# Projecting a whole batch ahead of attention, and putting the experts' spare tiles behind a branch

## The chip, the cores and the metric

One core of a Trainium2 chip runs one program. The metric is the device time of one execution in microseconds (us); less is better. Every time below comes from the runs or the profile of the kernel before.

## What is computed

The reference is one transformer layer with adaptive normalisation, for 4 sequences ("batches") of 2048 tokens with 256 channels, all in fp32:

```python
mod = (silu(c) @ wmod).reshape(4, 6, 1, 256)     # sa, ca, ga, sb, cb, gb; ga and gb at least 0.25 in size
h = layernorm(x) * (1 + ca) + sa
x = x + ga * attention(h)                        # 16 heads of 16 channels, rotary, causal softmax
h = layernorm(x) * (1 + cb) + sb
x = x + gb * moe(h)
# moe: sigmoid scores of 16 experts, the best 2 of 4 groups, the best 4 experts in them, weights scaled by 2.5;
#      y = sum over the 4 experts of w2(silu(w1 h) * (w3 h)) * weight, and a shared expert of the same shape (192 inner)
```

## The kernel before

**Attention.** Tokens go in blocks of 512, four to a batch (NQ = 4), 16 in all. For each block, `prologue(n)` normalises the rows of x, transposes them, multiplies by the modulation, projects to q, k and v (TensorE, PE), turns q and k by the rotary table, splits them into a high and a low part (fp32r) and stores them in DRAM (qd, kd, vd). A unit of attention is a block of queries with a group of 4 heads (`units`: 16 to a batch; the first batch has its units one by one, the later ones in pairs). For each unit `row_max` computes the scores once for the maximum of each row (VectorE, DVE, reduces them), and the main loop computes them again, transposed, in steps of 128 keys: PE (L1139, L1146), the exponential on ScalarE (ACT, L1154), on the diagonal a causal select on GpSimd (POOL, L1158), and the product with v on PE (L1087).

The order of instructions on PE, ACT, DVE and POOL is written out by hand; DMAs issued by SyncE (SP) are ordered by the framework. Everything beside the main loop is written as generators that yield what they need (a PSUM bank, DVE time, POOL time). The main loop pulls pieces of them between its steps, through queues (`Background`): `ahead` holds the prologues of blocks to come, at a rate set by `due`, so that a block is there when its first unit needs it; `maxes` the row maxima of the next unit; `ends` the output projection (`finish`); `after` the sending of finished blocks to the experts (`send`), and last `find_tiles`.

Only block 0 is projected at once, in an inner function `opening` of `prologue(0)`. Ahead of it stand the constants, the modulation and its rows (`rows`, `rowd`, L241 to L253) in a pool of their own, which is released before the pools of attention are filled. Blocks 1 to 3 go through `ahead`, beside the first units. Between the two, 32 regions of the buffers for the experts are filled with zeros (L1045, 272 KB each).

**Sending.** `send` normalises a finished block, routes it, and scatters each token's row to the regions of its four experts (L477). Experts work on tiles of 256 rows (TT), two tiles ("a pair") at a time, each tile of one expert; `find_tiles` counts the tiles and writes a table with each tile's expert and first row. There are two phases: blocks 0 to 11, whose experts' work may start when attention ends, and blocks 12 to 15, which are sent beside the first phase's pairs.

**Experts.** The number of pairs is fixed when the kernel is built, for the most padding that there can be, 255 rows an expert:

```python
self.pairs = -(-((4 * self.tokens + E * (TT - 1)) // TT) // 2)   # 56 in phase 0, 24 in phase 1
```

A pair that the table doesn't fill works on a repeated tile, and its results go to rows that nobody reads. Each pair loads 2 x 640 KB of weights (L1224) and 2 x 272 KB of rows (L1226), turns the rows (`turn`, L1240), multiplies up (`inner_a`, `inner_b`, L1255), takes silu times gate on ACT and DVE, multiplies down (`outer`, L1293 and L1304), scales by the weight and scatters four times 128 rows (`give`, L1358). Between these parts the loop pulls pieces of other work:

```python
def other(n):
    (late if m < split else rest).pull(n)      # called as other(2), other(1), other(2) for each pair
```

`late` is the sending of phase 1's blocks; `rest` (`back`) is, for all 16 blocks, the shared expert (`shared`, L1398) and, for the 12 blocks of phase 0, the sum of the four experts' results (`combine`, L1443 to L1450). After the last pair `rest` is drained, and the last four blocks are collected (L1386) and combined.

Of the kernel before, what the change touches and what calls it, by code (L numbers as in the profile page):

```python
# [118 lines left out]

@with_exitstack  # L120
def adaln_attention_moe(
# [33 lines left out]
    nc.sync.dma_start(gwT, gate_w)  # L155
    gbias = const.tile([P, E], F32, name="gbias")
    nc.sync.dma_start(gbias, gate_bias.partition_broadcast(P))
    bef = const.tile([P, E, E], F32, name="bef")
    nc.sync.dma_start(bef, before.partition_broadcast(P))

    sml = const.tile([P, 2 + len(PHASES), E], F32, name="sml")
    nc.sync.dma_start(sml, small.partition_broadcast(P))
    befb = const.tile([P, E, E], BF, name="befb")
    nc.vector.tensor_copy(befb, bef)
# [14 lines left out]
    for k, ph in enumerate(phases):  # L179


        ph.xs = dram.tile([E * ph.region, ROW], F32, name=f"xs{k}")

        ph.yd = dram.tile([4 * ph.tokens + 2 * ph.pairs * TT, D], F32, name=f"yd{k}")
        ph.first = sml[:, 2 + k, :]

        ph.run = const.tile([P, E], F32, name=f"run{k}")
        nc.vector.tensor_copy(ph.run, ph.first)
        ph.name = str(k)
# [16 lines left out]
    def gate(pool, g, name):  # L206

        sign = pool.tile(list(g.shape), F32, name=f"sign{name}")
        nc.vector.tensor_scalar(sign, g, 0.0, 2.0, ALU.is_ge, ALU.mult)
        nc.vector.tensor_scalar_add(sign, sign, -1.0)  # L210
        mag = pool.tile(list(g.shape), F32, name=f"mag{name}")
        nc.vector.tensor_scalar_mul(mag, g, -1.0)
        nc.vector.tensor_max(mag, mag, g)
        nc.vector.tensor_scalar_max(mag, mag, 0.25)
        nc.vector.tensor_mul(g, sign, mag)

    with tc.tile_pool(name="modw", bufs=1) as mw, tc.tile_pool(
        name="modp", bufs=1, space=PSUM
    ) as mp:
        wm = mw.tile([P, 2, 6 * D], F32, name="wm")  # L220
        nc.sync.dma_start(wm, wmod.rearrange("(k p) n -> p k n", p=P))
        sg = mw.tile([P, 2, B], F32, name="sg")
        nc.scalar.activation(sg, cT, AF.Sigmoid)
        nc.vector.tensor_mul(sg, sg, cT)
        pm = mp.tile([P, 4, B], F32, name="pm")
        for m in range(4):
            for k in range(2):
                nc.tensor.matmul(
                    pm[:, m, :],
                    lhsT=wm[:, k, m * P : (m + 1) * P],  # L230
                    rhs=sg[:, k, :],
                    start=(k == 0),
                    stop=(k == 1),
                )
        nc.vector.tensor_copy(mod, pm)
        nc.vector.tensor_scalar_add(mod[:, 2:4, :], mod[:, 2:4, :], 1.0)
        rows = mw.tile([B, 4, D], F32, name="rows")
        for m in range(4):
            pr = mp.tile([B, D], F32, name=f"pr{m}")
            for k in range(2):  # L240
                nc.tensor.matmul(  # L241
                    pr,
                    lhsT=sg[:, k, :],
                    rhs=wm[:, k, (2 + m) * D : (3 + m) * D],
                    start=(k == 0),
                    stop=(k == 1),
                )
            nc.vector.tensor_copy(rows[:, m, :], pr)
        nc.vector.tensor_scalar_add(rows[:, 2, :], rows[:, 2, :], 1.0)
        gate(mw, rows[:, 0, :], "a")  # L250
        gate(mw, rows[:, 3, :], "b")
        rowd = dram.tile([B, 4 * D], F32, name="rowd")
        nc.sync.dma_start(rowd, rows.rearrange("b m d -> b (m d)"))  # L253
# [8 lines left out]
    def normalise(xb, pools, xn):  # L262
# [11 lines left out]
        yield 0, 0, 0  # L274
# [22 lines left out]
    def route(lg, tp):  # L297
# [20 lines left out]
        def ranks(v, k, allowed):  # L318
# [20 lines left out]
            yield 0, 0, 0  # L339
# [32 lines left out]
    def send(n, xp, tp, psum, tag):  # L372
# [13 lines left out]
        for _ in range(3):  # L386
            yield 0, 0, 0
        h = yield from normalise(xb, tp, xb)
# [6 lines left out]
        yield 0, 0, 0  # L395
# [7 lines left out]
        yield 0, 0, 0  # L403
# [11 lines left out]
        re, ch, w = yield from route(lg, tp)  # L415
# [3 lines left out]
        yield 0, 0, 0  # L419
# [69 lines left out]
    tabs = ctx.enter_context(tc.tile_pool(name="tabs", bufs=1))  # L489

    def find_tiles(ph):
# [70 lines left out]
        nc.vector.tensor_scalar_add(tab[:, :, 2], tab[:, :, 2], -5.0)  # L562
        tabi = tabs.tile([P, 2, 3], I32, tag="tabi", name="tabi")
# [21 lines left out]
    with ExitStack() as actx:  # L585
# [24 lines left out]
        wqkv = acst.tile([P, 2, 3 * D], F32, name="wqkv")  # L610
        nc.sync.dma_start(wqkv, qkv_w.rearrange("(k p) n -> p k n", p=P))
        bqkv = acst.tile([P, 3 * D], F32, name="bqkv")
        nc.sync.dma_start(bqkv, qkv_b.partition_broadcast(P))
        wo = acst.tile([P, 2, D], F32, name="wo")
        nc.sync.dma_start(wo, out_w)
        ob = acst.tile([P, D], F32, name="ob")
        nc.sync.dma_start(ob, out_b.partition_broadcast(P))
        rp = acst.tile([P, T // P, 2, 2, HD // 2], F32, name="rp")
        nc.sync.dma_start(rp, rope)
# [12 lines left out]


        va_new = acst.tile([P, NG, 4, VG], F32, name="va")
        vh = va_new[:, :, :, : 4 * (HD + 1)].rearrange("p g t (h e) -> p g t h e", e=HD + 1)
        nc.gpsimd.memset(va_new, 0.0)
        for g in range(NG):
            nc.gpsimd.memset(vh[:, g, :, :, 0:1], 1.0)

        def prologue(n):  # L640
# [38 lines left out]
            def opening(hT, high_low, store):  # L679


                full = [P, 2 * H, 2, HD // 2]
                qks, rots = {}, {}

                def project(t):
                    ps = psp.tile([P, 2, BT], F32, tag="s", name="first")
                    for to, cols in ((ps[:, 0], slice(0, 2 * D)), (ps[:, 1, :D], slice(2 * D, 3 * D))):
                        for k in range(2):
                            nc.tensor.matmul(
                                to,  # L690
                                lhsT=hT[:, k, t * P : (t + 1) * P],
                                rhs=wqkv[:, k, cols],
                                start=(k == 0),
                                stop=(k == 1),
                            )
                    qk = ep.tile([P, 2, BT], F32, tag="e", name="qk0")
                    nc.vector.tensor_add(qk[:, 0], ps[:, 0], bqkv[:, : 2 * D])
                    nc.vector.tensor_add(
                        vh[:, :, t, :, 1:],
                        ps[:, 1, :D].rearrange("p (g h e) -> p g h e", g=NG, e=HD),  # L700
                        bqkv[:, 2 * D :].rearrange("p (g h e) -> p g h e", g=NG, e=HD),
                    )
                    qks[t] = qk

                def rotate(t):
                    qk = qks.pop(t)
                    parts = qk[:, 0].rearrange("p (h e two) -> p h e two", e=HD // 2, two=2)
                    prod = []
                    for s, eng in enumerate((nc.gpsimd, nc.vector)):
                        r_ = tp.tile(full, F32, tag=f"r{s}", name=f"r{s}", bufs=1)  # L710
                        eng.tensor_tensor(
                            r_,
                            parts[:, :, :, s].unsqueeze(2).to_broadcast(full),
                            rp[:, t, s].unsqueeze(1).to_broadcast(full),
                            ALU.mult,
                        )
                        prod.append(r_.rearrange("p h a e -> p h (a e)"))
                    xr = qk[:, 1].rearrange("p (h d) -> p h d", d=HD)
                    nc.vector.tensor_add(xr, prod[0], prod[1])
                    rots[t] = xr  # L720

                def split(t):
                    xr = rots.pop(t)
                    pt = wps.tile([P, 4, P], F32, tag="w", name="ptq")
                    for c_ in range(4):
                        nc.tensor.transpose(
                            pt[:, c_, :],
                            xr[:, 8 * c_ : 8 * c_ + 8, :].rearrange("p h d -> p (h d)"),
                            ident,
                        )  # L730
                    cols, whole = high_low(t, pt)
                    high, low = parts_[0]
                    lower(cols, whole, high, low)
                    if t % 2:
                        store(t // 2, high, low)

                project(0)
                project(1)
                rotate(0)
                project(2)  # L740
                for t in range(4):
                    if t < 3:
                        rotate(t + 1)
# [763 lines left out]
    for n in phases[1].blocks[:2]:  # L1507
        collect(n)
# [77 lines left out]
```

## Time and profile before

| | us |
|---|---|
| median of 3 runs (lowest, highest) | 3905.32 (3895.76, 3907.83) |
| the profiled execution's own time | 3907.39 |
| its span in the profile | 3905.7 |

Mean granted TensorE clock 0.901 of full speed. Busy shares of the span: PE 84%, DVE 66%, ACT 39%, POOL 39%.

| stretch of the span, us | what runs |
|---|---|
| 0 to 103 | constants, block 0, the first maxima, zeros |
| 103 to 901 | attention of batch 0, with the prologues of blocks 1 to 3 and then of the next batch |
| 901 to 1557, 1557 to 2231 | attention of batches 1 and 2, each with the next batch's prologues |
| 2231 to 2790 | attention of batch 3, no prologues left |
| 2816 to 3447 | the 56 pairs of phase 0, with the sending of blocks 12 to 15 |
| 3447 to 3860 | the 24 pairs of phase 1, with the shared expert and the sums of 12 blocks |
| 3860 to 3906 | the sums of the last four blocks |

The ends of batches are the last evictions of their units (L1097), those of the expert stages the first and last matmuls of their pairs. A profile shows one execution. A "wait" is the time that an engine sat idle before an instruction, and the name behind it is what released it. Lines are those of the kernel before.

### The profile page before, as it was taken

What the parts mean: (1) busy time and instruction counts of PE and PEld (TensorE: products, weight loads), DVE (VectorE), ACT (ScalarE), POOL (GpSimd) and SP (SyncE); (2) the same over time, 40 slices, a digit from 0 to 9 for tenths busy, and PEclk for the clock granted to TensorE, in tenths of its full rate; (3) what the DMA queues carried; (4) which work ended last, traced back from release to release, by engine and by line L of the source; (5) the groups of instructions that cost most, each with busy time, mean ns of one, the idle gap of its engine ahead of it and who ended that gap; (6) DMA issues with size and microseconds to landing.
All of it is one profiled execution on the core that took longest, in us unless ns stands there. A gap on an engine that the chain in (4) does not pass through costs nothing. (4 is left out here: it accounts for less than half of the span.)

```text
span 3905.7 us, 56489 instructions
## 1 busy us (share of the span) xinstructions
PE 3298.8 (84%) x20276; PEld 1723.2 (44%) x20400; DVE 2585.4 (66%) x4650; ACT 1525.6 (39%) x2188; POOL 1522.0 (39%) x2216
## 2 busy tenths in 40 slices
PE   3677988979889889888888988899888888899994
PEld 1333433434334333333433333333477676676662
DVE  2365776767776767766676777677276576667775
ACT  0233544544455544444444544455422222222220
POOL 1321243333433353244335334210155555545554
PEclk6688988989899988988988998899999898899997
DMA  5423232331333232223323322220377666688763
GB/s 163 144 84 120 98 131 101 121 118 63 109 110 123 96 117 93 81 84 102 123 101 117 104 72 71 101 96 1 114 255 242 205 226 236 216 280 303 273 248 140
DMA packets 279212, 544.96 MB, mean 140 GB/s; under 512 B 27535, under 2 KB 151439, under 8 KB 278931
## 3 DMA queue, kind: packets, MB, share of 16 engines
q1 hardware_dynamic: 249106, 461.61, 34.8%
q0 software_dynamic: 27648, 77.63, 5.3%
q8 instruction: 161, 2.64, 0.3%
q10 hardware_dynamic: 2176, 2.10, 0.2%
q14 instruction: 121, 0.98, 0.1%
HBM read 351.42 MB, written 189.81 MB: 139 GB/s over the span
## 5 line engine op out<-in xcount | busy, mean ns | idle before, releaser
L888 DVE TENSOR_REDUCE mparts<-ps 128x2 f32<-128x1024 f32 (+3 forms) x1152 | 1180.5, 1044 | 465.1 <-PE ps L878 421.1
L1154 ACT ACTIVATE e<-st 128x1024 f32<-128x1024 f32 (+3 forms) x1280 | 1078.6, 895 | 1031.3 <-PE st L1146 954.8
L878 PE MATMUL ps<-kt,qt 64*128 64x512 f32 (+3 forms) x3328 | 616.2, 415 | 187.2 <-ACT e L1154 64.8
L1087 PE MATMUL po<-e,vg 128*32 128x512 f32 (+3 forms) x5120 | 667.8, 588 | 27.4 <-POOL e L1158 15.7
L878 PEld LDWEIGHTS ps<-kt,qt 64*128 64x128 f32 x3328 | 304.7, 204 | 778.2 <-ACT e L1154 437.9
L1158 POOL TENSOR_SCALAR_AFFINE_SELECT e<-e 128x256 f32<-128x256 f32 x512 | 204.6, 410 | 964.6 <-ACT e L1154 960.7
L1255 PE MATMUL gu<-xT,wt 128*128 128x256 f32 x1920 | 462.9, 396 | 20.4 <-issue 9.5
L1358 POOL DMA_INDIRECT yd<-yt,to x320 | 315.9, 987 | 393.0 <-ACT hb L1266 200.3
L1146 PE MATMUL st<-qt,kt 64*128 64x512 f32 (+3 forms) x2560 | 461.4, 441 | 0.0
L1255 PEld LDWEIGHTS gu<-xT,wt 128*128 128x128 f32 x1920 | 370.4, 197 | 108.6 <-issue 44.0
L1139 PE MATMUL st<-mt,pick 32*128 32x512 bf16 (+3 forms) x2560 | 302.7, 375 | 74.0 <-DVE mparts L888 46.9
L477 POOL DMA_INDIRECT xs<-row,rowx x256 | 248.4, 970 | 175.0 <-DVE row L468 120.3
L911 DVE TENSOR_REDUCE mparts<-ps 128x8 f32<-128x1024 f32 x128 | 156.7, 1224 | 202.4 <-PE ps L878 191.6
L1146 PEld LDWEIGHTS st<-qt,kt 64*128 64x128 f32 x2560 | 206.1, 199 | 139.2 <-issue 127.5
L1354 ACT ACTIVATE yt<-y,of 128x256 f32<-128x256 f32 x160 | 67.1, 470 | 400.0 <-DVE is L1334 200.6
L803 POOL TENSOR_TENSOR r<-qk,rp 128x512 f32<-128x512 f32 x120 | 154.4, 1305 | 168.4 <-DVE qk L780 164.8
L1139 PEld LDWEIGHTS <-pick 32*128 32x128 bf16 x2560 | 86.9, 92 | 297.3 <-issue 285.3
L1087 PEld LDWEIGHTS po<-e,vg 128*32 128x32 f32 x5120 | 109.2, 112 | 185.8 <-issue 126.5
L749 POOL TENSOR_TENSOR low<-whole,high 128x512 fp32r<-128x512 f32 x64 | 81.4, 1271 | 258.9 <-ACT whole L676 258.7
L1293 PE MATMUL y<-wt,ha 128*128 128x256 f32 x640 | 161.7, 391 | 21.6 <-issue 18.5
L1293 PEld LDWEIGHTS y<-wt,ha 128*128 128x128 f32 x640 | 119.3, 196 | 41.8 <-issue 24.1
L776 PE MATMUL pq<-wqkv,hT 128*128 128x512 f32 x240 | 128.3, 660 | 10.4 <-ACT whole L676 8.6
(218 smaller groups left out, 3603.2 us busy)
## 6 DMA issues: line engine op xcount, KB each, us to landing
wt<-in_w_all SPq DMA_DIRECT2D x160, 640.0 KB
kt<-kd SPq DMA_DIRECT2D x124, 512.0 KB
xt<-xs SPq DMA_DIRECT2D x160, 272.0 KB
qt<-qd SPq DMA_DIRECT2D x64, 512.0 KB
yg<-yd SPq DMA_DIRECT2D x16, 2048.0 KB
vg<-vd SPq DMA_DIRECT2D x124, 168.0 KB
xb<-in_x SPq DMA_DIRECT2D x32, 512.0 KB
qd<-high SPq DMA_DIRECT2D x128, 128.0 KB
```

What stands on the lines that cost most here:

```text
L477: s_ = nc.gpsimd.indirect_dma_start(out=ph.xs[:, :], out_offset=bass.IndirectOffsetOnAxis(ap=rowx[:, n, t, j : j + 1], axis=0), in_=row[:, ...
L878: nc.tensor.matmul(ps[:, half, to : to + width], lhsT=qt[rows, q, t * P : (t + 1) * P], rhs=kt[rows, q, key : key + width], start=start, s ...
L888: nc.vector.tensor_reduce(to, ps[:, :, :width], AX.X, ALU.max)
L911: nc.vector.tensor_reduce(mine[:, :, :, 0], ps.rearrange("p h (t k) -> p h t k", k=P), AX.X, ALU.max,)
L1087: nc.tensor.matmul(po[32 * j : 32 * j + 32, off:], lhsT=va[:, k_, j * (HD + 1) : j * (HD + 1) + 32], rhs=es[j // 2][:, j % 2, off:], start ...
L1139: nc.tensor.matmul(sts[q][:, h_, off:], lhsT=pick[rows, :], rhs=mt[rows, off:], start=True, stop=False,)
L1146: nc.tensor.matmul(sts[q][:, h_, off:], lhsT=kt[rows, q, k_ * P : (k_ + 1) * P], rhs=qt[rows, q, off:], start=False, stop=True,)
L1154: nc.scalar.activation(es[q][:, :, off:], sts[q][:, :, off:], AF.Exp, scale=SCALE)
L1158: nc.gpsimd.affine_select(out=es[q][:, :, off : off + P], in_=es[q][:, :, off : off + P], compare_op=ALU.is_ge, fill=0.0, base=0, pattern= ...
L1255: nc.tensor.matmul(ps[:, c_ * TT : (c_ + 1) * TT], lhsT=wt[:, c_, k * 2 * I + cols : k * 2 * I + cols + P], rhs=xT[:, k, c_ * TT : (c_ + 1 ...
L1293: nc.tensor.matmul(pss[half][:, t, :], lhsT=ha[:, at_ : at_ + P], rhs=wt[:, half, 4 * I : 4 * I + D], start=(t == 0), stop=False, skip_gro ...
L1358: s_ = nc.gpsimd.indirect_dma_start(out=ph.yd[:, :], out_offset=bass.IndirectOffsetOnAxis(ap=to[:, t : t + 1], axis=0), in_=yt[:, t, :], i ...
```

## The change

1. **The opening.** `prologue(0)` with its inner function goes; a new generator `opening` projects all four blocks of batch 0 before attention, tile by tile of 128 rows. The modulation needs only the first half of `wm` for this; the rows of the gates (`modulation_rows`) are made in the middle of it (after tile 6), and the constants of the router are loaded behind it (`later_constants`). q and k are stored a block at a time, one half of the DMAs issued by SP, the other half by ACT. The maxima of the first unit are pulled beside the last two tiles.
2. **Zeros.** The 32 fills are no longer issued at once: `heads` queues them in `after`, each behind a tiny POOL write to the zeros.
3. **Pairs.** Each phase has `usual` pairs in the main loop (half a tile of padding an expert): 52 and 20, for 56 and 24. Every `find_tiles` keeps the number of tiles beyond that in `beyond`; at the end each engine reads it (`values_load`), and the remaining pairs, with all 16 blocks' shared expert and sums once more, lie in a `tc.If`.
4. **Pieces.** `send` in phase 1 and `shared` yield more often, so that dependent steps stand further apart, and the loop pulls 3, 2 and 2 pieces a pair in phase 0 and 5, 3 and 4 in phase 1, in place of 2, 1 and 2.

In `opening`, `project(i)` is four matmuls and two DVE adds out of PSUM; `rotate(i)` one product on POOL, one on DVE, and their sum on DVE; `split(i)` four transposes, two ACT copies and a difference on POOL. The diff, cut to its core:

```diff
+        self.usual = -(-(4 * self.tokens + E * TT // 2) // (2 * TT))
...
+        def store(n, cols, high, low, queues):
+            for c_ in range(4):
+                to = (qd, kd)[c_ // 2][n].rearrange("(h part d) t -> part h d t", part=4, d=HD)
+                to = to[:, 8 * (c_ % 2) : 8 * (c_ % 2) + 8]
+                for part in range(4):
+                    of = (high, low, *((high, low) if c_ < 2 else (low, high)))[part]
+                    queues[part % 2].dma_start(to[part][:, :, cols], of[:, c_, :].bitcast(F32))
+        def opening():
+            full = [P, 2 * H, 2, HD // 2]
...
+            wm = kvp.tile([P, 2, 6 * D], F32, tag="kt", name="wm")
...
+            nc.sync.dma_start(wm[:, :, : 2 * D], wms[:, :, : 2 * D])
+            fetch(0)
+            nc.sync.dma_start(wqkv, qkv_w.rearrange("(k p) n -> p k n", p=P))
+            nc.sync.dma_start(bqkv, qkv_b.partition_broadcast(P))
+            nc.sync.dma_start(rp, rope)
+            for n in range(1, NQ):
+                fetch(n)
+            nc.sync.dma_start(wm[:, :, 2 * D :], wms[:, :, 2 * D :])
...
+            def project(i):
...
+                ps = psp.tile([P, 2, BT], F32, tag="s", name="first")
...
+                nc.vector.tensor_add(qk[:, 0], ps[:, 0], bqkv[:, : 2 * D])
...
+            def rotate(i):
...
+                for s, eng in enumerate((nc.gpsimd, nc.vector)):
+                    r_ = tp.tile(full, F32, tag=f"r{s}", name=f"r{s}", bufs=1)
...
+                nc.vector.tensor_add(xr, prod[0], prod[1])
...
+            def split(i):
...
+                if t == 0:
+                    t_ = kvp.tile([P, 2, T], FR, tag="kt", name="hl")
...
+                nc.scalar.copy(high[:, :, cols], pt)
...
+                if t == 3:
+                    store(n, slice(0, BT), high, low, (nc.sync, nc.scalar))
...
+            run(normalise(xbs[0], tp, xbs[0]))
+            modulation()
+            turned(0)
+            run(normalise(xbs[1], tp, xbs[1]))
+            project(0)
+            project(1)
+            rotate(0)
+            project(2)
+            for i in range(4 * NQ):
+                n, t = divmod(i, 4)
+                if i + 1 < 4 * NQ:
+                    rotate(i + 1)
+                if t == 0 and n + 1 < NQ:
+                    turned(n + 1)
+                if i + 3 < 4 * NQ:
+                    project(i + 3)
+                split(i)
+                if t == 1 and n + 2 < NQ:
+                    run(normalise(xbs[n + 2], tp, xbs[n + 2]))
+                if i == 6:
+                    modulation_rows()
+                yield i
...
-        ahead.add(prologue(0))
-        ahead.drain()
...
+        for i in opening():
+            if i == 4 * NQ - 6:
+                load(0)
+                load(1)
+                maxes.add(row_max(*units[0][0]))
+            if i >= 4 * NQ - 2:
+                maxes.pull(2)
         maxes.drain()
         after_max.drain()
+        later_constants()
...
+        def heads():
+            for ph in phases:
+                for e in range(E):
+                    yield 0, 0, 0
+                    yield 0, 0, 0
+                    yield 0, 0, 0.1
+                    nc.gpsimd.memset(zeros[:, 0:1], 0.0)
+                    nc.sync.dma_start(
+                        ph.xs[e * ph.region : e * ph.region + TT, :].rearrange(
+                            "(p t) d -> p t d", p=P
+                        ),
+                        zeros.unsqueeze(1).to_broadcast([P, TC, ROW]),
+                    )
+        after.add(heads())
-        for n in range(1, NQ):
-            ahead.add(prologue(n))
...
+        many = small_tile("many", [P, 1])
+        nc.vector.tensor_scalar(many, last, float(1 - 2 * ph.usual), 0.0, ALU.add, ALU.max)
...
+    pairs = [(ph, i) for ph in phases for i in range(ph.usual)]
+    split, end = phases[0].usual, len(pairs)
+    pairs += [(ph, i) for ph in phases for i in range(ph.usual, ph.pairs)]
...
-        late.add(send(n, lp, lp, banks, "b"))
+        late.add(send(n, lp, lp, banks, "b", 3))
...
+        def other(k):
+            if m < split:
+                late.pull((3, 2, 2)[k])
+            else:
+                rest.pull((5, 3, 4)[k])
...
     rest.drain()
+    more_tiles = nc.values_load(beyondi[0:1, 0:1], min_val=0, max_val=E)
...
+    with tc.If(more_tiles > 0):
+        issued.clear()
+        for m in range(end, len(pairs)):
+            load(m)
+            turn(m)
+            ha = inner_a(wts_[m], xTs[m])
+            hb = inner_b(wts_[m], xTs.pop(m))
+            give(m, ha, hb)
+        for n in range(NB):
+            hT = fetch(n)
+            collect(n)
+            for gen in (shared(n, hT), combine(n)):
+                for _ in gen:
+                    pass
```

## The prediction

> **What bounds the kernel now.** I read the page first, then the windows by stage (row of a stage: stretch, its length, busy us of PE, weight loads, DVE, ACT, POOL with counts, granted clock, DMA share, GB/s):
>
> ```profile
> 103.00:901.00 798.00, 647.94 (x4133) 277.49 (x4162) 503.17 (x754) 330.07 (x430) 254.57 (x330) 0.87 0.33 111
> 901.00:1557.00 656.00, 585.48 (x3975) 248.04 (x4005) 471.75 (x713) 318.65 (x411) 257.28 (x368) 0.92 0.30 102
> 1557.00:2231.00 674.00, 593.73 (x3991) 254.41 (x4024) 476.71 (x738) 319.86 (x414) 266.80 (x379) 0.90 0.30 101
> 2816.00:3447.00 631.00, 547.21 (x2717) 439.00 (x2718) 414.01 (x1182) 160.22 (x344) 341.90 (x596) 0.92 0.69 235
> 3447.00:3860.00 413.00, 382.21 (x1681) 271.90 (x1679) 297.06 (x640) 90.31 (x204) 215.09 (x255) 0.97 0.71 260
> 3860.00:3906.00 46.00, 0.00 (x0) 0.00 (x0) 18.95 (x13) 0.00 (x0) 22.86 (x9) 0.53 0.37 137
> ```
>
> PE is the fullest engine of every stage but the last: 89% and 88% in batches 1 and 2, 87% in phase 0's pairs, 93% in phase 1's. Batch 0 stands out: 798 us for the same attention as 656 and 674, PE only 81% busy. The last 46 us hold no PE work. Then the costliest groups, for what a pair is made of, and the waits of PE in phase 0 (us in total, times, longest):
>
> ```profile
> L1255 PE MATMUL gu<-xT,wt 128*128 128x256 f32 x1920 | 462.9, 396 | 20.4 <-issue 9.5
> ```
> ```profile
> L1293 PE MATMUL y<-wt,ha 128*128 128x256 f32 x640 | 161.7, 391 | 21.6 <-issue 18.5 <-DVE ha L1267 3.0
> L1304 PE MATMUL y<-wt,hb 64*128 64x256 f32 x640 | 102.7, 414 | 14.0 <-issue 10.6 <-DVE hb L1268 2.9
> L1240 PE MATMUL ptx<-ident,xt 128*128 128x128 f32 x640 | 86.2, 277 | 14.0 <-DMA xt<-xs 12.4 <-issue 1.4
> ```
> ```profile
> PE pt L291 <- POOL row L392: 16.6, 7, 7.5
> PE pk L426 <- DVE ha L1267: 7.2, 1, 7.2
> ```
>
> A pair costs PE (462.9 + 161.7 + 102.7 + 86.2) / 80 = 10.2 us. The second waits belong to the sending of blocks 12 to 15: a transpose stands in PE's queue before POOL has its rows ready. Last the timelines of the opening and the tail.
>
> ```profile
> 53.17 1.73 DVE L719 TENSOR_TENSOR qk<-r,r 128x512 f32<-128x512 f32 x1 [2.53 <-POOL r L711]
> ```
> ```profile
> 53.09 1.26 POOL L749 TENSOR_TENSOR low<-whole,high 128x512 fp32r<-128x512 f32 x1
> 54.98 1.81 POOL L711 TENSOR_TENSOR r<-qk,rp 128x512 f32<-128x512 f32 x1 [0.63 <-DVE qk L719]
> ```
> ```profile
> 54.39 4.22 ACTq L762 DMA_DIRECT2D qd<-low  x4
> 63.76 0.59 ACTq L762 DMA_DIRECT2D kd<-high  x1
> 102.82 1.94 ACT L1154 ACTIVATE e<-st 128x1024 f32<-128x1024 f32 x2
> ```
>
> DVE's sum (0.69 us elsewhere) and POOL's product (1.31 elsewhere) stretch when they overlap; eight DMAs issued by ACT hold it from 54.39 to 64.35; the first exponential starts at 102.8.
>
> **1. The opening.** What it removes ahead of block 0: the gates' rows on DVE (17.3 to 23.4), then a wait to 25.4 for their store, because the next pools take that memory. Now the first DVE add (41.28 before) waits for the inputs ahead of block 1's rows: 512 + 512 + 768 + 384 + 256 + 512 = 2944 KB. Before, 2560 KB issued from 3.15 fed PE's first matmul at 11.9, so I put them at 15 to 16, and with a normalisation (29.5 to 34.5, 5 us) the first add at 21.
>
> From there a tile of 128 rows took (57.5 - 41.3) / 4 = 4.05 us before, its four tiles on DVE and POOL. Sixteen are 65; on DVE also two more normalisations (4 each) and the gates' rows (7): 80, to 101. PE has about 3.1 us of projection (12.22 / 4) and 0.6 to 1.1 of transposes a tile and stays below that. Each block's store makes ACT issue eight DMAs, 10 us in which it evicts nothing; PE then waits at the next transposes (one bank). Block 3's high part also takes the buffer whose store has just been issued. I count 6 us for each of the first three stores, and the last store's issue in full: first exponential at 101 + 18 + some 3 = 122, 19 later than now. Bounds: 105 (stores hidden by work already queued) and 150 (none hidden, 30 us, and the clock of 0.68 that the first 103 us were granted).
>
> The row above is what counts for the pace: POOL's 1.31 + 1.26 and DVE's 0.69 + 0.69 add up to 3.95, nearly the 4.05 seen, though they are on two engines. The Trainium skill ("SBUF — State Buffer", section "Who interferes with whom") says why: a Vector instruction with two SBUF inputs and a GpSimd instruction that reads SBUF exclude each other for a whole instruction. The trace agrees (1.73 us for a sum of 0.69). Without that rule one would take the busier engine alone, 2.57 us a tile, and the opening would end 24 us sooner.
>
> **2. Attention of batch 0.** It loses the prologues of blocks 1 to 3: each 18 us of PE (L776 8.6, L789 4.8, L817 2.8, transposes 1.9). The queue now only has the next batch's, as in batches 1 and 2, whose mean is 665. To that I add 15 for the four units of block 0 (23.5 us was the quickest of them, a tenth of a batch's work in proportion would be 17 a unit at most, and all their steps are diagonal) and 10 for the zeros: each POOL write waits for the fill before it, with a causal select queued behind it on POOL and PE's product with v behind that. A fill took 0.83 us in a row of 32 (26.7 us); alone it must go there and back, a few us, against steps of 5 to 6, so most is hidden; uncovered at 1.3 us each it is 40. Batch 0: 690 (655 to 720), to 122 + 690 = 812 instead of 901.5. **-90.**
>
> **3. Phase 0.** Four pairs at 631 / 56 = 11.3 us: 45, and 5 for PE's waits on the sending (about 24 in the rows above), whose steps now stand three pieces apart. **-50** (40, if only PE's 10.2 go, to 75).
>
> **4. Phase 1.** PE has 20 x 10.2 + 16 x 9.2 (the shared expert: L1398 5.5, L1293 2.2, L1304 1.6 a block) = 351 us, for 24 x 10.2 + 147 = 392 before. At the 93% of now that is 378 for 413: **-35** (20 to 45). Pieces: 14 a block for twelve blocks and 11 for four, 213 in all, at 12 a pair over 19 pairs, so nothing is left to drain.
>
> **5. The tail.** The 32 us after the last pair's matmuls (3828 to 3860) were filled by three blocks of the shared expert, and the last scatter and the collecting lay beneath. Now they are bare: scaling 1.5, four scatters 4.8, landing 2.4, collecting 8 to 9, then the sums as now, 45: 62 for 46. **+17** (5 to 25).
>
> **6. The branch.** Five reads of a register and five jumps. SP's issues with a read between them are 1.1 us apart of which 0.33 is the DMA, so a read is below 0.8; most engines do it while they wait for the collecting. The jump has no row here: between 0 and 10 I take **+2**, the nearer to the read. The Trainium skill ("Runtime: NRT & Kernel Launch", "Instruction fetch mechanics") speaks against the branch: a taken one whose target isn't fetched stalls for a DMA. By it this term would be nearer 10 and the sum 8 longer; no run here shows it yet.
>
> Sum against the profiled execution: 3907.4 - 90 - 50 - 35 + 17 + 2 = 3751; that execution lies 2 us above the median of the runs, so **3750**.
>
> **Rivals.**
>
> *The opening pays little.* Its tiles run at the pace of POOL and DVE together, and ACT's DMA issues come on top; the zeros hold POOL in the diagonal steps. For it: the stretched rows above, and the 14.75 us that ACT idled at 67 behind stores. Against: batches 1 and 2. With both upper bounds, 150 + 720 = 870: -31, and the experts' -66: 3810. Chance 0.22.
>
> *The experts gain more.* PE's waits in phase 0 vanish (75) and the shared expert fills phase 1 to its last pair (45): -101, with -90: 3716. Chance 0.13.
>
> *The branch is taken: slower.* Then eight pairs run bare and all blocks' sums twice. The price from the tail: three blocks' shared expert took 32 us, four sums 46: 22 a block, 350 for 16; a pair one after the other is 10.2 on PE and about 5 of silu and scaling: 120. 3750 + 470 = 4220. It decides from one tile beyond 104 in phase 0 or 40 in phase 1. The counts aren't in the trace; I worked them out from the reference's formulas and the inputs that it draws: 103 tiles and 40. Phase 1 is full to the last tile, but every expert with rows is at least 21 short of its next tile, and the three without any miss the last chosen score by 0.07 at the nearest token. The pairs left out are thus the empty ones. Chance 0.03. Another 0.02 for a slower result that I don't see (POOL held at every fill for over 5 us would do: 31 x 5 = 155).
>
> **How the numbers follow.** The forecast has 0.6. Its own range is 3720 to 3785. The range of 8 in 10 reaches to the rivals on both sides: 3700 to 3820. 0.3%, 12 us, is about what a measurement here can tell from no change: faster by more 0.94, within 0.01, slower 0.05.
>
> **What would show it.** First exponential near 122, and 16 projected tiles at 4 to 5 us before it with ACT empty during its DMA issues; the last eviction of batch 0 (L1097 before) near 812, batches 1 to 3 unchanged; 52 pairs in about 580 us, 20 in about 380; some 62 us from the last matmul to the end; 72 x 24 gate matmuls instead of 1920. Wrong if batch 0 ends later than 870, if a matmul stage falls below 85% busy, or if any line of the branch appears.

## The result, and the profile after

The changed kernel takes 3845.63 us (median of 4 runs, 3838.69 to 3858.31), the kernel before 3904.90 (4 runs): a ratio of 0.9853 (95% interval 0.9822 to 0.9883), 59 us faster. The prediction was 3750 with a range of 3700 to 3820: the sign was right, but of the 155 us forecast 59 came. The profiled execution of the changed kernel took 3858.31, the slowest of the four; its span is 3856.1. It is compared with the 3907.39 and 3905.7 of before.

First the windows by stage (the columns are those of the rows of before; the borders between the two phases of pairs lie where ACT copies the turned rows of a phase's first pair):

```profile
187.00:901.00 714.00, 607.39 (x3974) 255.98 (x4003) 483.94 (x715) 313.64 (x401) 219.47 (x350) 0.87 0.34 113
901.00:1556.00 655.00, 586.62 (x3966) 248.84 (x3998) 456.61 (x689) 318.46 (x411) 233.69 (x329) 0.91 0.29 98
1556.00:2220.00 664.00, 582.22 (x3988) 249.37 (x4020) 475.45 (x737) 319.41 (x412) 266.39 (x379) 0.92 0.30 101
...
2805.00:3418.00 613.00, 525.70 (x2579) 421.85 (x2579) 394.47 (x1132) 153.23 (x328) 330.31 (x572) 0.91 0.67 231
3418.00:3796.00 378.00, 339.27 (x1439) 236.19 (x1437) 268.81 (x548) 77.84 (x174) 191.44 (x206) 0.95 0.66 238
3796.00:3856.00 60.00, 0.00 (x0) 0.00 (x0) 17.32 (x15) 0.03 (x1) 24.88 (x19) 0.52 0.51 189
```

The first exponential starts at 186.72, 84 us later than before, and batch 0 then takes 714 us, 85 less: it ends at 900.75 where it ended at 901.53 (here and below, the end of a batch or a unit is the start of its last eviction). The forecast had it end at 812. The other 49 us of the profile come from batches 1 to 3 (10 us; traces of the same attention differ by more, 1863 to 1879 us for these three batches in the second group below) and from the experts: 1115.8 us from the last eviction of attention to the end before, 1077.1 now.

What fills the opening, from the timeline of ACT (start, duration; in brackets the idle time before and what ended it):

```profile
45.45 6.83 ACTq L634 DMA_DIRECT2D qd<-hl  x4
53.49 9.10 ACTq L634 DMA_DIRECT2D kd<-hl  x4
62.64 0.78 ACT L712 ACTIVATE aT<-pt,mod 128x512 f32<-128x512 f32 x1 [18.73 <-DMA kd<-hl]
...
109.44 0.78 ACT L712 ACTIVATE hT<-pt,mod 128x512 f32<-128x512 f32 x1 [17.13 <-DMA kd<-hl]
...
157.56 0.59 ACT L782 CAST hl<-ptq 128x512 fp32r<-128x512 f32 x1 [30.14 <-DMA kd<-hl]
...
184.71 0.59 ACT L1036 COPY mt<-pmx 128x512 bf16<-128x512 bf16 x1 [16.15 <-DMA qd<-hl]
```

And the waits of PE from 40 to 187 (in total, times, longest):

```profile
PE ptq L775 <- ACT whole L784: 28.6, 1, 28.6
PE pt L260 <- ACT aT L712: 19.8, 1, 19.8
PE pt L260 <- ACT hT L712: 18.6, 1, 18.6
PE st L1240 <- ACT mt L1036: 9.9, 1, 9.9
```

Four blocks, four holes: after each block ACT computes nothing for 16 to 30 us, 82 us in all. Its own 32 issues take 59.8 of them (the sum of its ACTq rows), and some 11 of the third hole come after its issues, in a wait for a buffer. PE stands behind ACT's evictions, DVE and POOL behind PE. Between the holes DVE finishes a tile every 3.6 to 3.8 us where nothing else stands in between (block 2, 120.2 to 131.3), close to the 4.05 counted.

### The profile page after: what moved, and what is told of

Read it like the earlier page. It is cut to its first block, busy times and chain, and to the rows that moved or that the text cites. A ratio compares the mean times of both kernels' runs of the same rounds, so it can differ in the third digit from the quotient of the medians.

```text
span 3856.1 us, 55123 instructions
## 1 busy us (share of the span) xinstructions
PE 3230.1 (84%) x19884; PEld 1672.2 (43%) x20008; DVE 2547.2 (66%) x4534; ACT 1506.2 (39%) x2140; POOL 1467.9 (38%) x2170
## 5 line engine op out<-in xcount | busy, mean ns | idle before, releaser
L1358 PE MATMUL gu<-xT,wt 128*128 128x256 f32 x1728 | 416.5, 397 | 14.4 <-DVE xT L1347 8.3
L1461 POOL DMA_INDIRECT yd<-yt,to x288 | 282.8, 982 | 334.2 <-ACT yt L1457 140.3
L1358 PEld LDWEIGHTS gu<-xT,wt 128*128 128x128 f32 x1728 | 333.4, 197 | 93.9 <-issue 36.2
L1247 PEld LDWEIGHTS st<-qt,kt 64*128 64x128 f32 x2560 | 205.3, 198 | 137.8 <-issue 125.9
L1396 PE MATMUL y<-wt,ha 128*128 128x256 f32 x576 | 152.8, 404 | 30.5 <-issue 27.1
L893 POOL TENSOR_TENSOR r<-qk,rp 128x512 f32<-128x512 f32 x96 | 124.0, 1307 | 96.4 <-DVE qk L870 96.4
L241 POOL TENSOR_TENSOR rs<-rs,mhalf 128x4 f32<-128x4 f32 x32 | 34.9, 1090 | 265.1 <-DVE rs L240 209.1
L1396 PEld LDWEIGHTS y<-wt,ha 128*128 128x128 f32 x576 | 110.9, 202 | 55.1 <-issue 38.5
L1370 DVE TENSOR_TENSOR hb<-hb,gu 64x256 f32<-64x256 f32 x144 | 59.3, 412 | 105.6 <-ACT hb L1369 79.7
```

Of the source, the lines that this page charges most:

```text
L1247: nc.tensor.matmul(sts[q][:, h_, off:], lhsT=kt[rows, q, k_ * P : (k_ + 1) * P], rhs=qt[rows, q, off:], start=False, stop=True,)
L1358: nc.tensor.matmul(ps[:, c_ * TT : (c_ + 1) * TT], lhsT=wt[:, c_, k * 2 * I + cols : k * 2 * I + cols + P], rhs=xT[:, k, c_ * TT : (c_ + 1 ...
L1396: nc.tensor.matmul(pss[half][:, t, :], lhsT=ha[:, at_ : at_ + P], rhs=wt[:, half, 4 * I : 4 * I + D], start=(t == 0), stop=False, skip_gro ...
L1461: s_ = nc.gpsimd.indirect_dma_start(out=ph.yd[:, :], out_offset=bass.IndirectOffsetOnAxis(ap=to[:, t : t + 1], axis=0), in_=yt[:, t, :], i ...
```

## The experiments

The comparisons ran on several chips. The kernel before takes 3825, 3821 and 3818 us in the first, third and fourth group below and 3907 in the second, which agrees with the chip of the result; so times are compared within a group, by the ratio to before. The other columns (us) come from one trace each.

| run (group) | first exponential | block 0's four units | batch 0 ends | attention's end to the end | ratio to before |
|---|---|---|---|---|---|
| before | 102.8 | 127.5 | 901.5 | 1115.8 | |
| changed | 186.7 | 84.5 | 900.8 | 1077.1 | 0.9853 (0.9822 to 0.9883) |
| sp_only (1) | 147.1 | 82.8 | 836.6 | 1028.2 | 0.9729 (0.9703 to 0.9756) |
| late_load (1) | 180.6 | 79.9 | 873.2 | 1025.5 | 0.9811 (0.9782 to 0.9839) |
| halves (1) | 168.4 | 78.2 | 858.7 | 1023.1 | 0.9768 (0.9741 to 0.9796) |
| experts_only (1) | 101.9 | 125.9 | 883.6 | 1026.1 | 0.9880 (0.9843 to 0.9917) |
| sp_split (2) | 118.3 | 98.0 | 843.1 | 1066.3 | 0.9724 (0.9697 to 0.9751) |
| no_fill (2) | 189.1 | 78.2 | 893.4 | 1074.8 | 0.9863 (0.9826 to 0.9901) |
| no_branch (2) | 187.8 | 76.0 | 893.7 | 1070.5 | 0.9856 (0.9826 to 0.9887) |
| old_pieces (2) | 186.7 | 81.9 | 890.0 | 1066.0 | 0.9869 (0.9843 to 0.9894) |
| opening_only (3) | 187.3 | 82.8 | 879.4 | 1064.0 | 0.9921 (0.9894 to 0.9949) |
| split_nofill (3) | 119.8 | 99.3 | 834.2 | 1021.7 | 0.9695 (0.9668 to 0.9722) |
| best (3) | 117.9 | 98.6 | 820.9 | 1020.8 | 0.9670 (0.9645 to 0.9695) |
| all16 (4) | 157.9 | 83.4 | 841.9 | 1021.2 | 0.9731 (0.9698 to 0.9763) |
| before16 (4) | 93.3 | 125.8 | 874.6 | 1062.2 | 0.9931 (0.9911 to 0.9951) |
| best16 (4) | 112.7 | 85.8 | 794.9 | 1016.2 | 0.9605 (0.9579 to 0.9630) |

### Who issues the stores

```diff
-                    store(n, slice(0, BT), high, low, (nc.sync, nc.scalar))
+                    store(n, slice(0, BT), high, low, (nc.sync, nc.sync))
```

> The changed kernel, with all DMAs of the opening's stores issued by SP, none by ACT. In the changed kernel ACT is held from 45.45 to 62.59, 93.69 to 109.40, 128.80 to 146.20 and 169.94 to 184.66 (67 us) by its 32 issues. Theory 1 (what costs the opening is that ACT stands in its own issues, which go at the pace of the bytes behind them, while PE waits for ACT's evictions): these holes go, up to what one block's 4 MB takes on one queue; first exponential near 135 (125 to 150) instead of 187, the end 40 to 50 us earlier than 3846, near 3800. Rival 1 (the bytes themselves bound it: 16 MB at the 187 GB/s of the holes, or one queue is slower than two): the third block's high part still waits for the buffer of the store before, first exponential 160 to 185 and the end 3825 to 3846. Rival 2 (an earlier first exponential is given back in batch 0, which would be bound by something else): first exponential at 135 but last eviction of batch 0 still within 15 us of 901.

Measured: 147.1, inside Theory 1's bounds, and a ratio 0.012 below the changed kernel's: 47 us. Three of the four holes are gone; one is left, in ACT's timeline:

```profile
127.14 0.58 ACT L782 CAST hl<-ptq 128x512 fp32r<-128x512 f32 x1 [38.22 <-DMA vd<-va]
```

So ACT's standing in its issues was the largest part, 40 us of the first exponential. SP alone issues a block's 16 stores in 19 us, ACT and SP together took 17. The Trainium skill ("Trainium Kernel Development and Optimization", "Key Constraints") says that issuing from several engines saves only issue time, because all queues share the same DMA engines; these two numbers agree with it.

### The order of the loads

```diff
-            if i == 4 * NQ - 6:
+            if i == 4 * NQ - 4:
                 load(0)
                 load(1)
```

> The changed kernel, with the loads of units 0 and 1 issued after the first tile of block 3 is split instead of two tiles earlier. They then take the buffers after block 3's high and low parts, which get block 1's... the ring of three is handed out in another order: block 3's parts take the buffer that block 0's parts had, whose store ended long before, and no longer the one whose store has just been issued. Theory 1 (ACT's 30.14 us of idleness to 157.56 is 17 us of issues and 11 to 13 of waiting for the store behind that buffer): the second part goes, first exponential 173 to 177, end 3833 to 3838. Rival (the wait is only pushed on: the loads now stand later in SP's queue and the first row maxima wait for them): first exponential stays within 4 us of 187.

The loads and the high and low parts of the blocks take turns in a ring of three buffers; the edit changes which of them block 3 gets. Measured: ACT's third idle time fell from 30.14 to 18.33 us, as Theory 1 has it, but the first exponential came only 6 us earlier, at 180.6, between the two forecasts: block 3's last tile now waited 7 us for its turn. The buffer was the cause of 12 us of that hole; half of that was pushed on.

### The same bytes in twice as many DMAs

```diff
-                if t == 3:
-                    store(n, slice(0, BT), high, low, (nc.sync, nc.scalar))
+                if t % 2:
+                    h_ = slice((t - 1) * P, (t + 1) * P)
+                    store(n, h_, high[:, :, h_], low[:, :, h_], (nc.sync, nc.scalar))
```

> The changed kernel, with each block's store split in two halves of 16 DMAs of 128 KB each, issued after its second and its fourth tile on the same two queues: twice the DMAs, the same bytes. Theory 1 (the issues go at the pace of the bytes): ACT is held about 8 to 9 us after each half, 67 us in all as before; first exponential 180 to 192, end 3840 to 3850. Rival (by number: each of ACT's issues costs its own time, 10 us for eight, as the sum of the prediction was made): 16 issues a block hold ACT twice as long, 20 us a block and more, first exponential 195 to 210. Rival (by burst: only what is issued in one go beyond a queue's room holds ACT): holes of 4 us or less, first exponential 150 to 165.

ACT's 64 issues took 61.1 us in all, the changed kernel's 32 took 59.8 (sums of its ACTq rows): the time goes with the bytes, not with the number. The forecast of the first exponential was missed all the same (168.4 for 180 to 192): the holes are now of 8 to 11 us, the one with the buffer of 17.6, and PE's waits for ACT's evictions add up to 68 us, 78 in the changed kernel. That short holes hide better beside work already queued is a reading of this, not tested by itself.

### The experts alone, and the front alone

Each is the kernel before with one part of the change; their diffs are not shown.

> The kernel before, with only the experts' part of the change: the usual pairs (52 and 20), the pieces and their spread, the branch. Opening and attention as before. Theory 1 (the gain of the changed kernel is this part alone): attention ends at 2790, end 37 to 47 us earlier than before, time 3858 to 3868. Rival (the part is worth the 66 us that the prediction gave, and the attention part costs some): 3835 to 3845.

> The kernel before with only the attention's part of the change: the first batch projected at once, the later constants, the paced zeros. Experts as before: 56 and 24 pairs, no branch. Theory 1 (experts_only carries nearly all of the gain, the front gives 0 to 12 us): ratio to before 0.996 to 1.001, attention ends at 2770 to 2785 where before ends at 2790. Rival (the two parts help each other, and the front alone is worth more or costs): outside 0.993 to 1.004. Phase 0's 56 pairs: 641 us, 11.45 a pair, if the chip is that of the traces of before and after; if its pairs take 10.8 as in experts_only, the phase is 605.

The experts' part gives 46 us of 3825 (by the interval 32 to 60), as Theory 1 said and not the 66 of the prediction. The front gives 30 us of 3821 (19 to 41), more than the 0 to 12 of Theory 1 and on the side of its rival; from a single pair of traces it had looked like 11. Traces of the two runs, on one chip, show where: in opening_only batch 0 ends 4 us earlier than in experts_only, which has the old front, and batches 1 to 3 take 1845 us instead of 1866 (1840 to 1857 in the five other traces of that chip with the new front). What shortens those batches was not tried. The two together would be more than the 59 of the result; both intervals are wide enough for that, and nothing more is read from it.

### The ring of buffers, and POOL's fills

sp_split is sp_only and this:

```diff
-            if i == 4 * NQ - 6:
+            if i == 4 * NQ - 4:
+                load(1)
+            if i == 4 * NQ - 6:
                 load(0)
-                load(1)
```

> sp_only, and besides the load of unit 1 is issued after the first tile of block 3 is split (that of unit 0 where it was), so that block 3's high and low parts take the buffer of block 1's, stored long before, instead of block 2's. In sp_only one hole was left on ACT in the opening, 38.22 us to 127.14, behind the store of block 2. Theory 1 (the opening's loss is the stores alone: first what holds ACT, then what holds the buffer): the hole goes, first exponential 112 to 122 (the prediction's 122), end another 20 to 30 us earlier than sp_only, ratio to before 0.965 to 0.968. Rival (SP's queue is the bound by now: it issues stores for 19 us a block, and the loads of unit 0 stand among them): first exponential 135 to 147, ratio 0.970 to 0.973.

The first exponential came at 118.3, inside Theory 1's 112 to 122, but the ratio is that of sp_only, 0.9724: both theories were half right. Block 0's units took 98 us instead of 83. PE's waits from 118 to 217, and POOL's timeline:

```profile
PE po L1189 <- POOL e L1260: 8.8, 1, 8.8
PE ps L968 <- DMA kt<-kd: 7.9, 1, 7.9
```
```profile
149.49 0.10 POOL L1147 MEMSET zeros<- 128x1 f32 x1 [15.40 <-DMA xs<-zeros]
149.54 0.77 POOL L1260 TENSOR_SCALAR_AFFINE_SELECT e<-e 128x256 f32<-128x256 f32 x2
```

What was won was given back to what stands behind the stores on SP's queue: the keys of unit 1, and a store of zeros on which POOL's next fill waits, with a causal select behind it. Two runs take the fill (`nc.gpsimd.memset(zeros[:, 0:1], 0.0)`) out, from the changed kernel and from sp_split:

> The changed kernel without POOL's fill of one column ahead of each store of zeros (the stores stay where they are; the fill only makes each wait for the one before). In the changed kernel POOL waited 42.0 us in 14 of these fills, between 189 and 372, with a causal select behind it. Theory 1 (the fills cost batch 0 part of the 24 us by which it was longer than predicted): first exponential to the last eviction of block 1, 228.6 us in the changed kernel, is 10 to 25 us shorter, ratio to before 0.979 to 0.983. Rival (the waits lie beside ACT's and PE's work, and the 24 us are the clock of 0.60 and the diagonal steps): under 5 us, ratio 0.984 to 0.987. Second rival (the stores then run as fast as they can beside the loads of units and delay these): longer.

> sp_split without POOL's fills. In sp_split the first exponential came at 118.31 but the four units of block 0 took 98 us, where they take 76 to 84.5 in the other runs: a fill waited 15.40 us to 149.49 behind the last store on SP's queue, a causal select behind it, PE 8.8 us behind that; and PE waited 7.9 us for unit 1's keys. Theory 1 (the gain was given back to the fill): block 0's units take 82 to 90 us, ratio to before 0.967 to 0.970. Rival (it is given back to the loads and stores themselves): 93 to 98 us, ratio 0.971 to 0.973.

In the changed kernel the fills cost nothing that can be seen: 219.7 us from the first exponential to the last eviction of block 1, but 220.1 and 222.4 in no_branch and old_pieces, which have the fills; ratio 0.9863. The rival holds. The changed kernel's own 228.6, at a granted clock of 0.80 in that stretch (0.86 in no_branch), is not the price of the fills: with the same fills the traces lie between 220 and 229. In split_nofill the ratio is 0.9695, the side of Theory 1, but block 0's units still take 99 us, which is the rival: PE now waits 15.7 us in two waits for keys.

### The branch, and the pieces

no_branch leaves out the `tc.If` with its body and the reads; old_pieces undoes the spread (`late.add(send(...))` without the 3, five pieces a pair, no extra yields in `shared`).

> The changed kernel without the branch and what lies behind it, and without the reads of its register; the table and its comparison stay. Theory 1 (the prediction: +2 us, not over 10): the last matmul to the end takes 57 to 60 us instead of 60.6. Rival (a branch over code that was not fetched stalls): 50 or less. Ratio to before 0.982 to 0.985.

> The changed kernel with the pieces of the sending and of the shared expert as before (5 a pair, waits of one piece), with the 52 and 20 pairs and the branch. Some four blocks of the shared expert are then left behind the last pair and cover its scaling, scatters and collecting, 46 us from the last matmul to the end instead of 60.6. Theory 1 (the finer spread is worth little, it was needed only because fewer pairs are there): attention to the end within 10 us of the changed kernel's 1077, ratio to before 0.983 to 0.988. Theory 2 (without the spread PE waits on the sending again, some 24 us, and four blocks run bare): 15 to 40 us longer, ratio 0.989 to 0.996. If phase 0 takes 586 us (11.27 a pair, as before) instead of 604, the spread itself is what slowed its pairs.

Without the branch the last matmul is followed by 58.1 us (one trace), with it by 60.6 to 62.1 in nine traces: about 3 us for the reads and the jumps together. Theory 1 holds. old_pieces has 47.7 us there, 609.5 us in phase 0 (610.8 in no_fill and no_branch) and the same ratio as the changed kernel within the intervals: the spread is worth nothing that these runs can tell, nor is it what slows phase 0.

### Bytes, or engines

```diff
-                to = (qd, kd)[c_ // 2][n].rearrange("(h part d) t -> part h d t", part=4, d=HD)
-                to = to[:, 8 * (c_ % 2) : 8 * (c_ % 2) + 8]
+                to = (qd, kd)[c_ // 2][n].rearrange("(h part d) t -> part h d t", part=4, d=HD // 2)
+                to = to[:, 16 * (c_ % 2) : 16 * (c_ % 2) + 16]
```

The rows of a head get another order, the same for q and k, so that their products add up to the same scores.

> The changed kernel with the rows of a head in DRAM (qd, kd) in another order, the same for q and k: two halves of 8 channels, each with its four parts. A store then writes 16 groups of 8 rows instead of 8 of 16; the bytes, the DMAs and the length of a row (2 KB) stay. Theory 1 (a DMA is spread over as many engines as divide its slowest dimension, 8 before and 16 now, and this, not the bytes, is why the issues of 4 MB hold ACT): DMA share in ACT's holes up from 0.5 to 0.6 to 0.8 or more, 8 issues by ACT take 8 to 10 us instead of 15 to 16, first exponential 140 to 155 instead of 187, ratio to before 0.972 to 0.978. Rival (the bytes bound it): as the changed kernel, 180 to 190, ratio 0.984 to 0.987.

> The kernel before with the rows' order of all16, nothing else. Its opening stores 2 x 2 MB. Theory 1: ACT's issues end some 5 us sooner, first exponential 94 to 100 instead of 102.8, and blocks 1 to 3, projected beside the units, are there a little sooner: ratio 0.995 to 0.999. Rival (the stores of all 16 blocks matter, by SP's queue): below 0.993.

Measured: four issues by ACT take 3.5 to 5.4 us instead of 5 to 9.5, its holes 10 to 12 us (17.6 the one with the buffer). The first exponential comes at 157.9, 3 us later than Theory 1 allowed, the ratio is 0.9731, inside its range, and the rival falls. The first store of the opening, while ACT issues its half, in the changed kernel and in all16:

```profile
45.45:62.59 17.14, 0.00 (x0) 0.00 (x0) 1.22 (x2) 0.00 (x0) 1.68 (x1) 0.50 0.56 190
46.67:57.52 10.85, 0.00 (x0) 0.00 (x0) 1.21 (x2) 0.00 (x0) 1.68 (x1) 0.50 1.00 315
```

The last two columns are the DMA engines' busy share and GB/s. Over the four stores they are 0.51 to 0.59 and 177 to 193 with eight groups of rows, 0.95 to 1.01 and 303 to 335 with sixteen. The kernel before gains too, 0.9931 (0.9911 to 0.9951), between its Theory 1 and the rival. The same on one queue: in sp_only a stretch in which every engine waits for the stores (first row), in best16, a version described below, a stretch of stores with work beside them; then SP's issues of block 0's stores in sp_only and in best16.

```profile
103.00:120.00 17.00, 0.00 (x0) 0.00 (x0) 0.00 (x0) 0.00 (x0) 0.00 (x0) 0.50 0.52 177
```
```profile
90.00:101.00 11.00, 4.91 (x24) 3.27 (x24) 9.56 (x11) 3.22 (x6) 8.23 (x6) 0.61 0.99 342
```
```profile
43.78 8.92 SPq L634 DMA_DIRECT2D qd<-hl  x8
52.74 10.04 SPq L634 DMA_DIRECT2D kd<-hl  x8
```
```profile
43.90 6.16 SPq L634 DMA_DIRECT2D qd<-hl  x8
50.10 6.27 SPq L634 DMA_DIRECT2D kd<-hl  x8
```

The bytes are the same, so it was not the bytes but the order of the rows. The Trainium skill ("DMA: Bandwidth & Descriptors", "Why a DMA increments its semaphore by 16 and not by 1") says that a DMA from SP or ACT runs on the largest number of engines up to 16 that divides the slowest dimension of both sides, so 8 here before the edit. The busy share of about a half, and its doubling, agree; which engines ran is not in these rows.

### The versions that beat both kernels

best is split_nofill, with the stores of zeros 20 steps later, the gates' rows worked out after the opening, and the pieces of old_pieces; best16 adds the rows' order.

> split_nofill, and besides: the zeros' stores start 20 steps later; the gates' rows (6 us on DVE in the middle of the opening) are worked out after it; the sending and the shared expert in the pieces of the kernel before, as in old_pieces (47.7 us from the last matmul to the end instead of 60.6). First exponential 108 to 116, block 0's units 76 to 84 us; the experts' part as in old_pieces. Ratio to before 0.960 to 0.967. Rival (loads behind stores hold the first units whatever is moved): 0.968 to 0.972.

> best with the rows' order of all16. Theory 1: SP issues a block's 16 stores in 9 to 12 us instead of 19; PE's two waits for unit 1's and 2's keys (16.6 us in best) go to under 6; block 0's units 80 to 88 us instead of 98.6; the stores of the later blocks are quicker too. Ratio to before 0.955 to 0.963. Rival (bytes): as best, 0.964 to 0.970.

best reaches 0.9670, the upper end of its forecast, but by the rival's mechanism: keys behind stores still hold the first units (16.6 us of PE's waits, 98.6 us for block 0's units, first exponential at 117.9). With the rows' order these waits are gone from PE's list, SP issues a block's stores in 12.4 us (9 to 12 expected), and best16 is at 0.9605 (0.9579 to 0.9630): 3668 us beside 3818 on one chip, 150 us less.

## Why the prediction was wrong, point by point

**1. The opening: this step failed, by 65 us.** Forecast 122, bounds 105 to 150, measured 186.7. The pace of the tiles was right: in sp_split, where ACT issues no store, the sixteen take from 18.3 (first add) to 106.5 (last sum), 88 us of which 7 are a wait behind a buffer's store, for the 80 counted. (That its first exponential, at 118.3, lies near the 122 is luck: the forecast has 18 us for stores, which ACT no longer issues there, and some 3 behind the last tile, where 12 passed.) The mis-sized term is "6 us for each of the first three stores, and the last store's issue in full". It came from the 10 us for which eight issues held ACT before, and took over the number of DMAs. But these moved 128 KB each and the new ones 256 KB, and the time goes with the bytes (halves). The words count the last store's issue in full, the sum has only some 3 us behind the 18; the last hole was 16. The buffer whose store has just been issued is named, but has no term: it was 12 us (late_load). The profile of before had the row from which it should have been sized:

```profile
54.00:66.00 12.00, 1.09 (x4) 0.72 (x4) 2.29 (x3) 0.00 (x0) 2.17 (x2) 0.50 0.56 176
```

That is a store of 2 MB at 176 GB/s; a block's 4 MB at that rate is 24 us, four of them 95, an estimate with nothing hidden. Measured were 82 us of holes, in place of the 18 and 3 of the sum. The DMA share of 0.56 beside a rate that the same profile exceeds elsewhere (305 GB/s at a share of 0.95, from 76 to 103) was a sign that the form of the stores was the limit, as all16 then showed.

**2. Batch 0: the mechanism was right.** 714 us, 703 to 706 in three traces of the second group (no_fill, no_branch, old_pieces) and 689 to 693 in four of a faster chip (sp_only, late_load, halves, opening_only), for a forecast of 690 within 655 to 720. Block 0's units took 84.5 us, for some 82 in the sum (a tenth of 665, and 15). The 10 us for the zeros are 0 (no_fill), so what the 24 us above the forecast are is not settled. That the batch ended after 870, the prediction's own sign of being wrong, comes from the opening.

**3. Phase 0: half of it.** From the first pair's turned rows to those of phase 1's first pair 641.3 us before and 612.9 now, -28 for a forecast of -50; on a faster chip 589.4 (opening_only) and 560.6 to 564.8, -25 to -29. The mis-sized term is the pair at 11.3 us, which is the mean of a stage with the sending in it. The last pairs of phase 0 before, after the sending, follow each other in 9.0 us: that is what a pair less saves, 36 for four. Of PE's waits on the sending 4 us went, for the 5 forecast: at `pt` and `pk` 28.4 us before, with the row that the prediction does not show (the first below), and 24.5 now (the other three):

```profile
PE pk L426 <- DVE chb L418: 4.6, 3, 2.0
PE pk L402 <- DVE chb L394: 9.9, 3, 5.1
PE pk L402 <- DVE ha L1370: 7.7, 1, 7.7
PE pt L260 <- POOL row L368: 6.9, 2, 5.8
```

That makes 40 for the 28 measured; where the other 12 went is not settled. PE's waits put down to "issue" rose from 40 to 47 us, and the granted clock was 0.91 in that stretch, 0.92 before.

**4 and 5. Phase 1 and the tail.** Together -11 (449.3 us to the end before, 438.2 now), forecast -18. The tail is 60.6 us from the last matmul, forecast 62. Phase 1 thus gained 25, within its 20 to 45, and not the 35. PE's busy time fell by 34 us (339 for 373), where 41 were counted (351 for 392), and its share did not stay at 93% but fell from 92% to 90%: the shared expert's second product waits for DVE, 30.6 us instead of 17.6:

```profile
PE y L1396 <- DVE sha L1517: 30.6, 9, 4.3
```

**6. The branch: right**, about 3 us for +2, and its body did not run; the groups show 72 x 24 gate matmuls:

```profile
L1358 PE MATMUL gu<-xT,wt 128*128 128x256 f32 x1728 | 416.5, 397 | 14.4 <-DVE xT L1347 8.3
```

The Trainium skill ("Runtime: NRT & Kernel Launch", "Instruction fetch mechanics") says that a taken branch whose target isn't fetched stalls for a DMA. The prediction allowed 10 us for that; these runs do not show it.

**The rivals.** "The opening pays little" had the right mechanism, ACT's issues on top, and 3810, nearer to the result than the forecast; the zeros that it also named cost nothing (no_fill). Even its upper bound of 150 was 37 us short, since it scaled the same wrong row. With the rows' order in both kernels the change is worth more: all16 against before16 is 3718.55 to 3793.11, 75 us.

## What to carry to other kernels

Size a DMA issue that holds an engine by the bytes behind it at the rate which the trace shows for that form of transfer, not by the number of issues; where the DMA share stays near a half while everything waits for it, count the groups of rows that a transfer is cut into. Price a removed iteration by the interval between two undisturbed ones, not by the mean of its stage (36 us for four pairs here, 28 came). And after an earlier start has been won, look at what stands behind the same transfers on the same queue: 29 us of sp_split's earlier exponential brought almost nothing until the keys came in time.

## What the runs showed of the hardware

One store ran at 177 to 193 GB/s (changed kernel) or at 303 to 335 GB/s (all16) by the order of rows in DRAM alone, with the same bytes and rows of 2 KB.

Chips differ, by 2% for the kernel before (3905 to 3907, and 3818 to 3825), and most of what the traces show of it is in one stage: sp_split on the slower and split_nofill on a faster one, which differ in POOL's fills alone, are 67 us apart, 43 of them in phase 0. There PE is busy for 521 and 499 us, at granted clocks of 0.91 and 0.94, which is 22 of the 43. The 52 pairs of phase 0 take 603 to 613 us on the slower chip and 558 to 565 on the faster ones, phase 1 to the end 431 to 439 on all. In the changed kernel PE waits 47 us in phase 0 for nothing that the profile shows ("issue"); in sp_only, on a faster chip, its list of waits there has none of that kind. A stretch of it, while POOL issues one scatter after the other (PE's timeline of the changed kernel):

```profile
2925.51 0.58 PE L1407 MATMUL y<-wt,hb 64*128 64x256 f32 x1 [2.22 <-issue]
2928.30 0.58 PE L1407 MATMUL y<-wt,hb 64*128 64x256 f32 x1 [2.22 <-issue]
2930.41 0.58 PE L1407 MATMUL y<-wt,hb 64*128 64x256 f32 x1 [1.52 <-issue]
```

One matmul in 2 to 3 us, with ACT and DVE idle too. Why was not tried.
